# A graph layer's sparse sums: a ring of sums by edge type, with the weights applied when nodes leave it

## The chip, the cores and the metric

The kernel runs on one core of a Trainium2 chip. The metric is the device time of one execution, in microseconds (us). The engines are PE (TensorE: matrix products), DVE (VectorE), ACT (ScalarE), POOL (GpSimd, which here issues the indirect gathers) and SP (SyncE, which issues the plain DMAs). PEld is the loading of weights into PE. SBUF is the on-chip memory, of 128 partitions; PSUM holds PE's results, in banks that a pool hands out in turn.

## The reference

One layer of a typed graph network, cut to what matters:

```python
# x [12500, 128]; src, dst, edge_type [200000], edges sorted by dst
# W [4, 128, 128]; b [4, 128]
h = relu(layernorm(x))
xs = h[src]
for i in range(4):
    msgs += where(edge_type == i, xs @ W[i] + b[i], 0)
out = x + segment_sum(msgs, dst, N)
```

The destinations are drawn as the square of a uniform number, times 12500: the first nodes have hundreds of edges each, the last ones about eight.

## The kernel before, in words

**The table.** The kernel normalises x and stores h as a table `htab` in DRAM, as three bf16 pieces a row (384 bf16 values: `D3`), so that three bf16 products together carry an f32 value. This takes the first 99 us of the trace.

**Edges.** The 200000 edges, in order of destination, make 1563 chunks of 128. They are treated in three ways.

- *Dense.* The first 512 chunks (`C0`) belong to the first few hundred nodes. For them, `count` makes a matrix "how many edges go from this table row to this node and type": for each slot, DVE makes two one-hot matrices, `o1` (lines 943 and 947) and `o2` (line 948, 392 columns), PE multiplies them (line 959) and ACT writes the counts as fp8 (line 962). `multiply` then multiplies the whole table with the counts (line 999; the table comes in blocks of `HB` = 4 node columns, tile `hs`, through SP's queue), and its tail applies W and adds to `acc`, an SBUF array for the first 11 blocks of 128 nodes. There are 14 such batches, and the generator `dense_work` hands the work out in small steps.
- *Raw.* The first 3 groups (`RAW`) of 16 chunks after those are gathered from x itself (line 522) and normalised on the spot, while the table is still being made.
- *Sparse.* The other 1003 chunks come in groups of `G` = 16, with small groups of 12, 8, 4 and 3 at the end. POOL gathers 128 rows of the table per chunk with an indirect DMA (line 538, tile `hm`, two chunks to a buffer, 20 buffers). DVE makes a one-hot matrix `oh` (line 555) from type and destination: 4 types times a window of `win` destination nodes (10 to 26, growing along the edges, since later nodes have fewer edges).

**The sum of a sparse group** (`sum_up`, then `weigh`). Three matmuls a chunk (line 572: the three pieces of `hm` against `oh`) give, for the chunk, the sum of its rows by type and by node of the window. ACT copies these sums to SBUF (line 575). PE counts the edges by type and node (line 590), ACT casts the counts (line 594), and PE puts bias times counts (line 597) and W times sums, one f32 product per type over the whole group (line 599), into one PSUM bank. From there DVE adds each chunk's `win` columns into the ring (line 660), an SBUF array of `RING` = 2048 node columns (and 32 more for what hangs over), at an offset that is read from memory at run time.

**Nodes that leave.** When no later edge can reach a node block any more (`due`, `goes`), `put_out` empties it: `leave` fetches x for four blocks (`OT` = 4) by SP, transposes the ring's columns on PE (line 685), adds on DVE, stores through SP (line 694), and clears the ring's columns with a memset. The first 11 blocks go from the ring into `acc`, and leave at the end of the dense work.

**The order of the work.** PE, DVE and ACT run in the order in which the program is written out (`manual_schedule`). The loop over groups takes each group in parts of two chunks (`HG`). After each part, as much dense work is issued as `pace` says, by columns of PE work (`columns` estimates a group's), so that dense work lasts till nearly the end of the full groups. One-hots of the next group and ring additions of the group before (`side`) are dealt out over the parts. In `count`, one-hots are made `AHEAD` = 8 slots ahead of PE, from pools of 12 buffers each. Gathers of a group are issued one group ahead, on POOL's queue, as far as buffers are free.

Of the kernel before, what the change touches and what calls it, by code (L numbers as in the profile page):

```python
# [28 lines left out]

# [19 lines left out]
P = 128  # L49
EPS = 1e-5  # L50
UN = 3
G = 16
# [6 lines left out]
HB = 4  # L59
AHEAD = 8  # L60
BEHIND = 0.06
RING = 2048
OT = 4
# [3 lines left out]
SOON = (RAW * 16) + HG  # L67

# [4 lines left out]
def kernel(  # L73
# [148 lines left out]
    ring = const.tile([P, RING + WIN], F32, name="ring")  # L222
# [7 lines left out]
    hpool = mid.enter_context(tc.tile_pool(name="rows", bufs=20))  # L230
# [3 lines left out]
    s_ps = mid.enter_context(tc.tile_pool(name="s_ps", bufs=2, space=PSUM))  # L234
    y_ps = mid.enter_context(tc.tile_pool(name="y_ps", bufs=1, space=PSUM))
# [236 lines left out]
    banks = [(s_ps, "ps"), (s_ps, "ps"), (y_ps, "py"), (a_ps, "pa")]  # L472
# [87 lines left out]
    finish = []  # L560
    flushing = []

    def sum_up(t0, g, rows, oh, last):
        win = window_of(C0 + t0)
        K = NT * win
        sb = spool.tile([P, G * KM], F32, name="sb")[:, : G * K].rearrange("p (g t n) -> p g t n", g=G, t=NT)
        for i0 in range(0, g, SG):
            i1 = min(i0 + SG, g)
            ps = s_ps.tile([P, 512], F32, name="ps")[:, : SG * K].rearrange("p (i n) -> p i n", i=SG)
            for i in range(i0, i1):  # L570
                for c in range(3):
                    nc.tensor.matmul(ps[:, i - i0, :], rows(i, c), oh[:, i, :], start=(c == 0), stop=(c == 2))  # L572
                if i % HG and i + 1 < i1:
                    yield (i + 1) / g
            nc.scalar.copy(sb[:, i0:i1].rearrange("p g t n -> p g (t n)"), ps[:, : i1 - i0, :])  # L575
            yield i1 / g

        finish.append(weigh(t0, g, oh, sb, last))

    def weigh(t0, g, oh, sb, last):  # L580
        win = window_of(C0 + t0)

        def bank():
            to = x_ps.tile([P, G * WIN], F32, name="pt") if last else y_ps.tile([P, G * WIN], F32, name="py")
            return to[:, : G * win].rearrange("p (g n) -> p g n", g=G)

        ohv = oh.rearrange("p g (t n) -> p g t n", t=NT)
        pc = bank()
# [6 lines left out]
        yield True  # L595
        py = bank()
        nc.tensor.matmul(py[:, :g, :], b128, cnt[:, :g, :], start=True, stop=False)
        for t in range(NT):
            nc.tensor.matmul(py[:, :g, :], wsb[:, t, :], sb[:, :g, t, :], start=False, stop=(t == NT - 1))  # L599
# [873 lines left out]
```

## Time and profile before

| what | value |
| --- | --- |
| median of 3 runs | 1405.44 us (1405.35 to 1410.56) |
| the profiled execution's own time | 1402.26 us |
| its span in the profile | 1400.5 us |
| PE busy | 1314.0 us (94%) |
| DVE busy | 1002.7 us (72%) |
| ACT busy | 628.8 us (45%) |
| POOL busy | 1032.2 us (74%) |
| gathers of table rows (line 538) | 1003, mean 972 ns |
| one-hots `o2` (line 948) | 1167, mean 333 ns |
| table times counts on PE (line 999) | 4116, 892.2 us |
| sums of rows on PE (line 572) | 3009, 186.6 us |
| W on the sums (line 599) | 488, 130.7 us |
| copies of the sums on ACT (line 575) | 251, 100.3 us |
| ring additions on DVE (line 660) | 976, 167.8 us |

The profile records one execution. Busy time is the sum over an engine's instructions, so an engine can be busy without setting the pace, and an instruction's busy time can hold time in which it waits for the one ahead in its pipeline. Slices are 40 equal parts of the span, with busy shares in tenths. A line of the view of waits names who waited, behind the arrow what ended the idle time (the releaser; "issue" means that the engine waited for nothing that the profile shows), and then the idle time in us, how often, and the longest one. A line of the view by stretches has the stretch, its length, busy us and number of instructions of each engine (or of one program line alone), and at the end the clock granted to PE (1.00 is full), the DMA engines' busy share and GB/s. A line of the timeline has start, duration, engine, program line, operation, its tiles and, in brackets, the idle time before it and its releaser.

### The profile page before, as it was taken

The page shows a single profiled execution, that of the slowest core. Times are in us where ns is not written, and L with a number is a line of the kernel's source. Part 1 is how long each engine was busy: PE and PEld are TensorE (multiplying, and loading weights), DVE is VectorE, ACT ScalarE, POOL GpSimd, SP SyncE. Part 2 cuts the span into 40 slices and gives each one's busy share as a digit, 9 for nine tenths or more (in the row PEclk, how much of TensorE's full clock was granted, in tenths as well). Part 3 has the DMA queues.
Part 4 walks back from the last instruction along what each step waited for, and adds up shares of the span by engine and source line. Part 5 has one row for each costly group of instructions (what it writes and reads, how often), then busy time and mean ns, then how long its engine had stood idle before and what let it go on. Part 6 is the DMA issues. An engine that isn't in the chain of part 4 may idle for free.

```text
span 1400.5 us, 30850 instructions
## 1 busy us (share of the span) xinstructions
PE 1314.0 (94%) x9776; PEld 809.6 (58%) x9776; DVE 1002.7 (72%) x5153; ACT 628.8 (45%) x2043; POOL 1032.2 (74%) x1078
## 2 busy tenths in 40 slices
PE   4869888999999999999999999999999999999974
PEld 1437466565666666666666656666666655556543
DVE  9990999987887678776767767676777667753533
ACT  6795626244263535445353543535344353361111
POOL 7726777777777777777777777777777777777774
PEclk9995899999999999999999999999999999999977
DMA  8643466676667767676767666777677666767752
GB/s 249 220 172 81 115 193 204 182 219 172 202 186 217 213 202 213 204 220 198 212 190 222 199 202 201 207 208 208 187 208 206 193 199 184 207 189 205 215 146 68
DMA packets 143094, 270.27 MB, mean 193 GB/s; under 512 B 26602, under 2 KB 79004, under 8 KB 142925
## 3 DMA queue, kind: packets, MB, share of 16 engines
q1 hardware_dynamic: 93245, 166.45, 39.0%
q0 software_dynamic: 49680, 101.81, 26.8%
q8 instruction: 77, 1.26, 0.4%
q14 instruction: 92, 0.75, 0.2%
HBM read 252.12 MB, written 16.04 MB: 191 GB/s over the span
## 4 chain that ended last, share of the span: by engine, by line
PE 77%; DVE 10%; DMA 6%; issue 3%; POOL 2%; ACT 1%; SPq 0%; DVEq 0%; POOLq 0%; ACTq 0%
PE pa L999 45%; PE pt L959 12%; PE py L599 8%; PE ps L572 6%; DMA hm<-htab,srcT 5%; DVE o L948 2%; POOL hm L538 2%; DVE o L947 1%; PE ps L629 1%; DVE oh L555 1%; DVE ring L660 1%; DMA hm<-in_x_dram 1%; PE pt L685 1%; PE py L590 1%; PE pt L1015 1%
## 5 line engine op out<-in xcount | busy, mean ns | idle before, releaser
L538 POOL DMA_INDIRECT hm<-htab,srcT x1003 | 974.5, 972 | 332.6 <-issue 190.4
L999 PE MATMUL pa<-counts,hs 128*128 128x416 fp8e4 (+1 forms) x4116 | 892.2, 337 | 0.6 <-ACT sd L1009 0.6
L999 PEld LDWEIGHTS <-hs 128*128 128x128 bf16 x4116 | 391.4, 98 | 257.6 <-issue 1.9
L962 ACT ACTIVATE counts<-pt 128x392 uint16<-128x392 f32 x714 | 355.4, 507 | 342.6 <-PE pt L959 326.1
L948 DVE TENSOR_SCALAR o<-iota_n,hkT 128x392 bf16<-128x392 f16 x1167 | 388.1, 333 | 0.0
L959 PE MATMUL pt<-o,o 128*128 128x392 bf16 x1167 | 372.6, 334 | 10.1 <-DVE o L948 7.0
L555 DVE TENSOR_SCALAR oh<-iota_b,keyT 128x56 bf16<-128x56 bf16 (+8 forms) x1003 | 173.2, 264 | 185.4 <-PE py L590 182.6
L660 DVE TENSOR_TENSOR ring<-ring,py 128x14 f32 (+7 forms) x976 | 167.8, 172 | 95.5 <-PE py L599 46.2
L575 ACT COPY sb<-ps 128x224 f32<-128x224 f32 (+8 forms) x251 | 100.3, 400 | 295.4 <-PE ps L572 278.7
L572 PEld LDWEIGHTS <-hm 128*128 128x128 bf16 x3009 | 162.0, 98 | 101.2 <-DMA hm<-htab,srcT 28.9
L572 PE MATMUL ps<-oh,hm 128*128 128x56 bf16 (+8 forms) x3009 | 186.6, 197 | 23.4 <-DMA hm<-htab,srcT 21.5
L959 PEld LDWEIGHTS <-o 128*128 128x128 bf16 x1167 | 113.0, 98 | 78.9 <-DVE o L948 15.0
L947 DVE TENSOR_SCALAR o<-iota_b,loT,byT 128x128 bf16<-128x128 bf16 x417 | 139.6, 335 | 12.2 <-PE pt L959 10.4
L962 ACT ACTIVATION_READ_ACCUMULATOR counts<-pt 128x1 f32 x714 | 147.1, 206 | 0.0
L599 PE MATMUL py<-sb,wsb 128*128 128x224 f32 (+7 forms) x488 | 130.7, 412 | 0.0
L943 DVE TENSOR_SCALAR o<-iota_b,loT 128x128 bf16<-128x128 bf16 x375 | 98.2, 262 | 13.0 <-PE pt L959 12.7
L599 PEld LDWEIGHTS py<-sb,wsb 128*128 128x128 f32 x488 | 89.3, 196 | 25.3 <-issue 2.9
L947 DVE TENSOR_SCALAR o<-iota_b,loT 128x128 bf16<-128x128 bf16 x375 | 97.1, 259 | 8.2 <-PE pt L959 7.9
L522 POOL DMA_INDIRECT hx<-in_x_dram,srcT x48 | 52.1, 1086 | 19.6 <-issue 9.6
L594 ACT CAST cnt<-py 128x224 bf16<-128x224 f32 (+7 forms) x61 | 24.2, 396 | 56.6 <-PE py L590 56.6
L455 ACT ACTIVATE h<-hm,nmrt,rstdt 128x128 f32<-128x128 f32 x98 | 43.1, 502 | 0.8 <-DVE nmrt L450 0.5
L484 PE MATMUL ps<-h,ident 128*128 128x384 f32 (+1 forms) x34 | 16.7, 575 | 16.1 <-ACT h L455 16.0
(230 smaller groups left out, 601.8 us busy)
## 6 DMA issues: line engine op xcount, KB each, us to landing
hs<-htab SPq DMA_DIRECT2D x336, 384.0 KB
hm<-htab,srcT POOLq DMA_INDIRECT x1003
htab<-h SPq DMA_DIRECT2D x32, 288.0 KB
xo<-in_x_dram SPq DMA_DIRECT2D x23, 256.0 KB
out_dram<-xo SPq DMA_DIRECT2D x23, 256.0 KB
hm<-in_x_dram SPq DMA_DIRECT2D x18, 192.0 KB
hs<-htab SPq DMA_DIRECT2D x14, 192.0 KB
hm<-in_x_dram SPq DMA_DIRECT2D x14, 168.0 KB
```

The costliest lines, as they stand in the source:

```text
L538: one = nc.gpsimd.indirect_dma_start(out=hm[:, (i - h0) * D3 : (i - h0 + 1) * D3], out_offset=None, in_=htab, in_offset=bass.IndirectOffse ...
L555: nc.vector.tensor_scalar(oh[:, i, :], iota_b[:, :K], keyf[:, at : at + 1], None, ALU.is_equal)
L572: nc.tensor.matmul(ps[:, i - i0, :], rows(i, c), oh[:, i, :], start=(c == 0), stop=(c == 2))
L575: nc.scalar.copy(sb[:, i0:i1].rearrange("p g t n -> p g (t n)"), ps[:, : i1 - i0, :])
L599: nc.tensor.matmul(py[:, :g, :], wsb[:, t, :], sb[:, :g, t, :], start=False, stop=(t == NT - 1))
L660: nc.vector.tensor_tensor(to, to, of(i), ALU.add)
L943: nc.vector.tensor_scalar(o1, iota_b, loT[:, s : s + 1], None, ALU.is_equal)
L947: nc.vector.tensor_scalar(o1, iota_b, loT[:, s : s + 1], by, ALU.is_equal, ALU.mult)
L948: nc.vector.tensor_scalar(o2, iota_n, hkT[:, s : s + 1], None, ALU.is_equal)
L959: nc.tensor.matmul(pb, o1, o2, start=first, stop=last)
L962: nc.scalar.activation(counts[:, :, i * NT : (i + 1) * NT], pb.rearrange("p (b t) -> p b t", t=NT), AF.Copy, accum_out=both[:, i : i + 1],)
L999: nc.tensor.matmul(pa[:, : nv * NT], hs[:, j - j0, c * D : (c + 1) * D], counts[:, j, : nv * NT], start=(j == 0 and c == 0), stop=(j == NW ...
```

## The change

- The ring holds, for every node, the sums of h by type (4 planes) and the summed bias (a fifth plane), instead of one finished sum: `ring` becomes [128, 5, 1024 + 32] instead of [128, 2048 + 32].
- W is no longer applied to each group (`weigh` and its lines 590 to 599 go, with the copy of line 575). It is applied when a block leaves the ring: `from_ring` multiplies the block's four planes with the four W and the fifth with the identity, into one PSUM tile that stands where the transpose's result stood. Blocks leave in twos (`OT` = 2), at most one such pair per group, at the part `FLUSH` = 3.
- Bias times counts goes into the same PSUM bank as the chunk's sums (five planes of `win` columns a chunk). The counts of a group (`counts_of`) are made in the group before.
- DVE adds the five planes of a chunk with one instruction, straight from PSUM, two parts after PE has made them (`LAG` = 2). The pool of these banks gets a third bank; the bank for W's results goes.
- Row buffers: 16 pairs instead of 20.
- In `count`, one-hots lie in tiles of 4 slots (`SLOTS`), 4 tiles per kind, each made while the set two before it is multiplied; ring additions and one-hots of rows are dealt out between the steps of dense work, instead of behind all those of the part.
- The table is loaded in blocks of 7 node columns (`HB` = 7) in 3 buffers, instead of 4 in 4.
- `columns`, which feeds `pace`, counts the new work. The clearing of the ring covers five planes. The check of counts of a batch is dealt out in steps. The order at the end of the program is written anew.

The core of the diff:

```diff
-HB = 4
-AHEAD = 8
+HB = 7
+SLOTS = 4
-RING = 2048
-OT = 4
+RING = 1024
+OT = 2
+LAG = 2
+FLUSH = 3
...
-    ring = const.tile([P, RING + WIN], F32, name="ring")
+    ring = const.tile([P, NT + 1, RING + WIN], F32, name="ring")
...
-    hpool = mid.enter_context(tc.tile_pool(name="rows", bufs=20))
+    hpool = mid.enter_context(tc.tile_pool(name="rows", bufs=16))
-    s_ps = mid.enter_context(tc.tile_pool(name="s_ps", bufs=2, space=PSUM))
-    y_ps = mid.enter_context(tc.tile_pool(name="y_ps", bufs=1, space=PSUM))
+    s_ps = mid.enter_context(tc.tile_pool(name="s_ps", bufs=3, space=PSUM))
...
+    def counts_of(t0, g, oh):
...
+        nc.scalar.copy(cnt[:, :g], pc[:, :g])
+        return cnt
+
+    def sum_up(t0, g, rows, oh, cnt):
+        win = window_of(C0 + t0)
+        many = SG if SG * (NT + 1) * win <= 512 else HG
+        banks = []
+        each = ring_adds(
+            t0,
+            g,
+            lambda i: banks[i // many][0][:, i - banks[i // many][1]],
+            lambda at: ring[:, :, bass.ds(at, win)],
+        )
+        for i0 in range(0, g, many):
+            i1 = min(i0 + many, g)
+            ps = s_ps.tile([P, 512], F32, name="ps")[:, : many * (NT + 1) * win]
+            ps = ps.rearrange("p (i k n) -> p i k n", i=many, k=NT + 1)
...
+                if i % HG and i + 1 < i1:
+                    yield (i + 1) / g
+            nc.tensor.matmul(ps[:, : i1 - i0, NT, :], b128, cnt[:, i0:i1, :], start=True, stop=True)
+            banks.append((ps, i0))
+            adds.append(each[i0:i1])
+            yield i1 / g
...
+    def from_ring(j, r, to):
+        c = j * P % RING
+        for t in range(NT):
+            nc.tensor.matmul(to, ring[:, t, c : c + r], wsb[:, t, :], start=(t == 0), stop=False)
+        nc.tensor.matmul(to, ring[:, NT, c : c + r], ident, start=False, stop=True)
...
             if again:
-                nc.vector.memset(ring[:, c0 : c0 + n], 0.0)
+                nc.vector.memset(ring[:, :, c0 : c0 + n], 0.0)
...
+        for n, of in enumerate(sets):
+            while len(making) < min(n + 3, len(sets)):
+                making.append(make(sets[len(making)]))
+                made.append([])
+            ahead = [m for m in range(n, min(n + 2, len(sets)))]
+            for m in ahead:
+                made[m] += list(making[m])
+            for k, (i, s, by, first, last) in enumerate(of):
+                if n + 2 < len(sets) and len(made[n + 2]) < len(sets[n + 2]):
+                    made[n + 2].append(next(making[n + 2]))
...
-        return sizes[gi] * (3 * max(64, K) + 5 * K)
+        nodes = N * (((C0 + starts[gi] + sizes[gi]) / T) ** 2 - ((C0 + starts[gi]) / T) ** 2)
+        return sizes[gi] * (3 * max(64, K) + K + win) + 4 * (NT + 1) * nodes
...
-    hsp = counting.enter_context(tc.tile_pool(name="hsp", bufs=4))
+    hsp = counting.enter_context(tc.tile_pool(name="hsp", bufs=3))
...
+            flush = j == FLUSH and out_now
+            if flush:
+                while ready and ready[0][0] <= last_add:
+                    ready.pop(0)[1]()
+            lag, many = (LAG, HG) if gi < FULL else (1, SG)
+            some = [ready.pop(0)[1] for _ in range(many) if not flush and ready and ready[0][0] + lag <= at_part]
...
             while work and spent < pace(gi, part):
                 spent = next(work, None)
                 if spent is None:
                     work = None
+                if some:
+                    some.pop(0)()
...
+            if flush:
+                ending.append(put_out(*out_now.pop(0), True))
+            while adds:
+                ready.extend((at_part, add) for add in adds.pop(0))
```

## The prediction

> **What bounds the kernel now.** I read the page's busy shares and slices first, then the busy times by stretch, then who POOL waits for, then counts by line, then the timeline at the end.
>
> ```profile
> PE 1314.0 (94%) x9776; PEld 809.6 (58%) x9776; DVE 1002.7 (72%) x5153; ACT 628.8 (45%) x2043; POOL 1032.2 (74%) x1078
> PE   4869888999999999999999999999999999999974
> POOL 7726777777777777777777777777777777777774
> ```
>
> PE looks like the bound: nine tenths or more from slice 8 on. POOL looks idle a quarter of the time. The stretches show what that quarter is.
>
> ```profile
> 400.00:450.00 50.00, 50.00 (x405) 30.84 (x404) 38.84 (x210) 26.78 (x96) 38.13 (x40) 1.00 0.71 204
> 1000.00:1050.00 50.00, 50.00 (x377) 30.74 (x376) 36.60 (x187) 20.86 (x69) 38.12 (x40) 1.00 0.69 200
> 1300.00:1350.00 50.00, 44.32 (x317) 26.66 (x314) 25.45 (x149) 6.71 (x14) 37.84 (x40) 0.97 0.68 193
> ```
>
> Columns: length, then PE, PEld, DVE, ACT, POOL, each with its count. POOL issues 40 gathers in every 50 us, one in 1.25 us, also at the end where PE is no longer full. POOL's waits say that nothing holds it:
>
> ```profile
> POOL hm L538 <- issue: 190.4, 625, 0.3
> POOL hm L538 <- ACT rstdr L446: 21.5, 1, 21.5
> POOL hm L538 <- ACT hx L455: 8.0, 7, 4.6
> ```
>
> Of 1003 gathers nearly all have a gap of 0.3 us, whatever name it bears. Only the first (21.5 us, until the table is stored) and two more (1.9 and 4.6 us, held to the raw groups) really wait. From the first gather at 99.46 us to the last at 1384.18 us there are 1002 spacings of 1.25 us (1252 us), 6 us of those two waits, and 27 us of stretch (the group's mean of 972 ns against 945 ns, times 1003): 1285 us, all of the time there is. Gathers (first fence) and row matmuls, three a chunk (second), from the start to four moments:
>
> ```profile
> 0.00:270.00 270.00, 126.00 (x128) 0.89 0.59 176
> 0.00:400.00 400.00, 225.54 (x228) 0.93 0.62 183
> 0.00:860.00 860.00, 575.54 (x589) 0.97 0.67 195
> 0.00:1130.00 1130.00, 780.95 (x801) 0.97 0.68 197
> ```
>
> ```profile
> 0.00:270.00 270.00, 16.16 (x300) 14.95 (x300) 0.89 0.59 176
> 0.00:400.00 400.00, 32.50 (x612) 30.09 (x612) 0.93 0.62 183
> 0.00:860.00 860.00, 96.10 (x1734) 87.37 (x1734) 0.97 0.67 195
> 0.00:1130.00 1130.00, 138.39 (x2388) 124.36 (x2388) 0.97 0.68 197
> ```
>
> POOL is 28 chunks ahead of PE at 270 us, 24 at 400, 11 at 860, 5 at 1130: PE catches up long before the end, and from there waits for rows. The end is POOL's queue plus a tail:
>
> ```profile
> 1384.18 0.94 POOL L538 DMA_INDIRECT hm<-htab,srcT  x1 [0.30 <-issue]
> 1387.21 0.31 PE L572 MATMUL ps<-oh,hm 128*128 128x104 bf16 x3 [0.96 <-DMA hm<-htab,srcT]
> 1389.07 1.96 PE L599 MATMUL pt<-sb,wsb 128*128 128x78 f32 x8
> 1395.05 0.41 SPq L694 DMA_DIRECT2D out_dram<-xo  x1
> ```
>
> **The change part by part.** The profiled execution took 1402.26 us (span 1400.5); the median of the runs is 3.2 us above it. The sum is made against the first.
>
> W on leaving nodes, on PE. Removed: the L599 matmuls, 143 thousand columns over their forms; eight of 256 columns go from 706.82 to 708.55 us, 0.84 ns a column: 120 us. Removed too: 87 transposes (L685, four in 0.50 us): 10 us. Added: 87 blocks with ten f32 instructions each (W for four types and the identity, two passes each). Nearest row: L1015, 104 columns, eight in 0.88 us, 0.11 us each: 96 us. The bias goes from 61 wide matmuls (about 0.11 us) to some 250 narrow ones (0.033 us, as L572's 72 columns): +1 us. Net 33 us less PE work, 0.5 us a group of 16. What covers it is the gather queue: PE only catches up sooner. It is worth nothing to the end; it adds to a margin, since PE now gains about 0.7 us a group on POOL and reaches it some ten groups early.
>
> ACT loses 251 copies (L575, 100 us); ACT is 45% busy and off the path: 0.
>
> DVE. Each ring addition grows from win to 5 win columns. L660 takes 164 ns for 10 columns, L1025 210 ns for 58: about 1 ns a column, so 955 additions x 72 columns give +70 us. The clearing memsets grow from 20 of 512 columns (485 ns) to about 43 of up to 1280 (1408 columns took 1.23 us): +35 us. Against this the waits of oh for L590 (183 us) go, since the counts are made a group ahead. 1003 us becomes about 1110: no bound over the whole, but from 150 to 266 us DVE has no idle time at all. There it decides how far PE lags, and the row buffers fall from 20 to 16 pairs: POOL may be 32 chunks ahead, not 40. In this trace a limit of 16 would leave 2.5 us of slack at the tightest gather (the 114th), 4 to 6 us up to the 190th. I summed DVE's queue up to the one-hot that each chunk's matmuls stand behind, by start-to-start spacings of this trace (o2 0.231, o1 0.16 or 0.22, oh 0.142; a ring addition 0.202 behind another one, 0.08 behind another kind, plus 1.04 ns a further column). For the kernel before, this is within 2 us of the trace up to 270 us. For the changed order, where additions stand singly between one-hots, it comes 3.4 us later at chunk 16, 1 us at 64, 2 us at 96, 3 us at 128. Bounds: 0, and 7 us if single additions cost as much as those in a row (chunks then 6 to 11 us late, less the slack). I take +1, nearer the isolated rows.
>
> The stretch of the gathers. It comes with o2 (L948) alone: gathers with none starting beside them last 3 ns over 945, with one 21, two 39, three 105; runs of ring additions do nothing. In the built order, 750 of 885 runs of o2 are of one; before, most are of two and more (up to 19, as at 331 to 337 us, where gathers take 1.27 us). The count, 1167, stays. At 20 ns each that is 23 us instead of 27. Bounds: -10 (the o2 hardly meet gathers) and +5 (DVE, no longer held by L590, runs ahead and bunches). I take -3.
>
> [...]
>
> POOL's queue: the ring's memset goes from 2080 to 5280 columns (1.82 to about 4.6 us) and delays the 48 raw gathers; they end at 78 us, with 21.5 us idle after: 0; without that cover, 2.8 us. The raw groups get a third sum bank: they waited 2.3 us in all for copies, so the two held gathers may come sooner: between -2 and 0; I take -1.
>
> SP's queue: table loads of 7 blocks instead of 4 (350 loads become 196, same bytes), 45 fetches and 45 stores instead of 24. In the built order a load is released at least 8 us of PE work before its first use (6.5 us before), for 672 KB instead of 384 KB: at the 200 GB/s of the stretches 3.4 us instead of 1.9. No wait of PE for hs is in this trace; I take 0, bounds 0 and the margin below. Two fetches of x now stand ahead of the last table stores: their wait ends with a slot matmul (L851, last at 65.4 us), so they cost issue time, 0.43 us each; between 0 and 1, I take +0.5.
>
> The wait that is added: PE's flush stands behind DVE's additions of the group before, and DVE's clearing behind PE's flush. The first are emitted a part (2.5 us) or more earlier; behind the second stand one-hots that PE needs some three parts later: 0.
>
> The tail. Before, 7.8 us pass from the last rows (1387.2) to the last store. Removed: W, counts and copy of the last group (1387.4 to 1390.8). Added: 40 f32 matmuls for blocks 92 to 95, able to start at about 1384.5, ending 1388.9 (0.11 us each); the last rows' matmuls 0.7; five DVE additions, 1.9; 20 f32 matmuls, 2.2 us at full clock or 4.3 at half (L599's 78-column rows: 0.21 us); 0.5 for DVE. The store goes out at 1394.2 to 1396.5; with the 40 at half clock too, up to 4 us later. I take +1; bounds -1 and +5.
>
> Sum: +1 -3 -1 +0.5 +1 = -1.5 us: 1400.8 for the profiled execution, 1404 for the median.
>
> **The rivals.** *PE is the bound after all.* Then its 33 us come off: 1372. For it: 50.00 of 50. Against: POOL's rhythm is the same where PE has idle time. 0.05.
>
> *The stretch goes.* If spreading o2 takes most of the 27 us, 1385 or so; the gathers with no o2 show it possible, the constant count speaks against. If half goes, 1391. 0.11 for the two.
>
> *Sixteen pairs are too few* (the other side). If DVE between 140 and 300 us falls behind by more than the slack, POOL waits for a free buffer and never regains it. By additions at the price of a row it costs 7 us (1412); it decides over 0.5% from a lag of about 11 us at chunks 80 to 150. For it: DVE has no idle time there, and a ring addition has five times the columns. 0.14.
>
> *New waits eat PE's margin.* PE could lose about 40 us (33 plus what is left at 1130 us) before it bounds again; late loads of hs at each of 14 batches, 5 us each, give 70: 1435. 0.06. *The tail at half clock* with small losses elsewhere: 1413. 0.04.
>
> *The lock.* If single o2 each held a gather for half their length, 1167 x 0.76 (POOL's share) x 0.115 us = 102 us against 27: 1480. The gathers with one o2 now (21 ns) speak against. 0.02. [...]
>
> **How the numbers follow.** 0.5%, 7 us, is about what a measurement of this kernel tells from no change. The forecast, POOL's queue as before, holds 0.58, and all of it lies within 0.5%. Faster: 0.05 + 0.11 = 0.16. Slower: 0.14 + 0.06 + 0.04 + 0.02 = 0.26. The forecast's own bounds (-13 to +18 with every end at once) make 1397 to 1413 likely. The range of 1390 to 1418 takes in half of the stretch rival below, and the buffers' and the tail's above; it leaves out 0.05 + 0.05 + 0.06 + 0.02 = 0.18.
>
> **What would show it.** POOL still 40 gathers in 50 us, the last at about 1382 to 1386 us; PE idle in many slices, waiting for hm, from about 700 us; L599 and L575 gone, some 870 f32 matmuls at the flush; the group mean of L538 below 972 ns. Wrong would be: spacings of POOL over 1.3 us named after PE between 200 and 320 us (buffers), PE waits for hs, or a first gather later than 101 us.

## The result, and the profile after

The changed kernel takes 1418.1 us (median of 5 runs, 1416.4 to 1421.5) against 1405.4 us before: 1.0088 times as long, with a 95% interval of 1.0071 to 1.0105. Measured side by side a second time, it was 1.0091 (1.0069 to 1.0112). The forecast was 1404.0 us, no change beyond 0.5%; the time is 1% above it, and 0.1 us above the range given. The profiled execution took 1418.36 us, its span is 1416.6 us. In 8 of the 18 runs below, called stalled, every kernel took about 1.2 times as long (the one before 1680 to 1705 us), because the queue of gathers stopped 230 to 248 times for about 1.3 us, for a reason that no run shows; of these runs only counts within one trace and comparisons among themselves are used.

Lines of the program move a little: the gathers are L540 now, the row matmuls L592, the ring additions L662, the clearings L728, o2 L971. From the page of the changed kernel: busy times, and the slices of PE and POOL.

```profile
PE 1293.5 (91%) x10240; PEld 813.9 (57%) x10240; DVE 1056.5 (75%) x5250; ACT 547.2 (39%) x1792; POOL 1042.0 (74%) x1078
PE   4979888999999999999999999999999989999675
POOL 7626777777777777777777777777777777777773
```

PE has 20 us less to do, DVE 54 us more, ACT 82 us less. The prediction had PE stand in many slices waiting for rows; it is still at nine tenths. The same stretches as before, with the same columns:

```profile
400.00:450.00 50.00, 48.62 (x406) 29.60 (x405) 40.66 (x218) 24.39 (x86) 38.12 (x40) 1.00 0.66 206
1000.00:1050.00 50.00, 49.07 (x410) 31.57 (x408) 40.34 (x201) 15.61 (x53) 38.41 (x39) 1.00 0.64 197
1300.00:1350.00 50.00, 37.48 (x296) 23.84 (x295) 31.42 (x165) 0.96 (x2) 37.81 (x41) 0.87 0.63 197
```

POOL keeps its rhythm, with one gather missing between 1000 and 1050 us. PE now has holes: 12.5 us of them in the last line. Gathers and row matmuls (three a chunk) from the start to the four moments:

```profile
0.00:270.00 270.00, 124.59 (x128) 0.89 0.58 178
0.00:400.00 400.00, 223.31 (x230) 0.92 0.59 183
0.00:860.00 860.00, 574.79 (x586) 0.96 0.63 195
0.00:1130.00 1130.00, 780.87 (x796) 0.97 0.63 196
```

```profile
0.00:270.00 270.00, 16.30 (x306) 15.04 (x306) 0.89 0.58 178
0.00:400.00 400.00, 32.09 (x606) 29.58 (x606) 0.92 0.59 183
0.00:860.00 860.00, 94.98 (x1716) 85.61 (x1717) 0.96 0.63 195
0.00:1130.00 1130.00, 137.12 (x2370) 121.78 (x2370) 0.97 0.63 196
```

POOL leads by 26 chunks at 270 us, 28 at 400, 14 at 860, 6 at 1130. With 33 us less work PE was to catch up sooner than before (28, 24, 11, 5); it catches up later, although POOL is 5 gathers behind its old place at 1130 us. The waits, in us, times, longest:

```profile
POOL hm L540 <- issue: 221.2, 726, 0.3
PE ps L592 <- DVE ring L662: 50.9, 52, 2.7
POOL hm L540 <- ACT hx L457: 28.6, 8, 22.0
```

In the kernel before, PE's row matmuls waited for ring additions 1.2 us in all, and its matmuls of the counts (L590) 8.6 us:

```profile
PE ps L572 <- DMA hm<-htab,srcT: 21.5, 25, 3.1
PE py L590 <- DVE ring L660: 8.6, 4, 3.2
PE ps L572 <- DVE ring L660: 1.2, 2, 1.0
```

There PE waited 21.5 us for rows. Among the waits of the changed kernel's row matmuls none is for rows (3.9 us in its second trace): PE stays behind POOL to the end, and its own delay sets the end.

POOL is late as well, and its account closes: the first gather starts at 102.18 us (+2.7), the two early waits are 1.1 us shorter, the gathers are stretched by 36.2 us over 945 ns each instead of 26.7 (+9.5), the last one starts at 1395.32 us instead of 1384.18 (+11.1). From it to the end 21.3 us pass instead of 16.3 (+5.0). Together +16.1 us, the difference of the spans.

The stretch has two parts. From the starts and durations of the gathers and of the clearings (L728): 26 gathers that start while a clearing runs, or up to 0.22 us ahead of it, are stretched by 20.3 us together, the longest by 1.38 us; in the kernel before, no gather was stretched by more than 0.05 us under a clearing (8 started there). All other gathers are stretched by 16.0 us, against 26.7 us before. The timeline of one held gather, and of one that is not (start, duration, engine, line):

```profile
955.53 2.30 POOL L540 DMA_INDIRECT hm<-htab,srcT  x1 [0.30 <-issue]
...
955.71 1.12 DVE L728 MEMSET ring<- 128x1280 f32 x1 [0.21 <-DVE xo L690]
956.76 0.26 DVE L731 TENSOR_TENSOR ring<-ring 128x160 f32<-128x160 f32 x1
...
896.50 1.12 DVE L728 MEMSET ring<- 128x1280 f32 x1 [0.22 <-DVE xo L690]
897.66 0.26 DVE L662 TENSOR_TENSOR ring<-ring,ps 128x100 f32 x1
...
896.94 0.95 POOL L540 DMA_INDIRECT hm<-htab,srcT  x1 [0.30 <-issue]
```

The two clearings are alike (40 of the 42 have 1280 columns, two have 640). What differs is the DVE instruction behind them. At 956.76 it is the fold, recorded as starting 0.08 us before the clearing ends, so it was already lined up; the gather lasts 2.30 us. At 897.66 it is a ring addition, which waits for the clearing by a semaphore and starts 0.03 us after its end; the gather beneath lasts 0.95 us. (It differs in kind too: one of its operands lies in PSUM. These rows alone do not tell waiting from kind; the runs below do in part.) This divides all 42 clearings, each of which has a gather starting under it or just ahead of it: with an o2 (L971) next, 16 of 16 are held; with the fold next, 10 of 10; with a ring addition next, 0 of 16. And the end tells which instruction lets go: behind a clearing with an o2 next, the gather ends 0.945 us after a moment 13 to 22 ns before the clearing's end; with the fold next, 42 to 47 ns after it. The o2 ends 117 ns after the clearing, the fold 177 ns: the same 60 ns.

The holding begins while the wide instruction still stands behind its predecessor. The gather at 955.53 would, with its 0.945 us, have ended at 956.48, 0.28 us before the fold is recorded as starting; in 9 of the 26 that end would come ahead of the wide instruction's recorded start, by up to 0.31 us. What it is in the chip that holds the gather, no run shows.

At the end, the timeline after:

```profile
1395.32 0.94 POOL L540 DMA_INDIRECT hm<-htab,srcT  x1 [0.30 <-issue]
1396.10 0.62 DVE L662 TENSOR_TENSOR ring<-ring,ps 128x130 f32 x2 [0.42 <-PE ps L601]
1396.77 2.07 PE L704 MATMUL pt<-wsb,ring 128*128 128x128 f32 x8 [0.71 <-DVE ring L662]
1403.89 0.44 PE L592 MATMUL ps<-oh,hm 128*128 128x104 bf16 x6
1404.19 0.30 PE L592 MATMUL ps<-oh,hm 128*128 128x104 bf16 x3
1409.62 0.50 SPq L694 DMA_DIRECT2D out_dram<-xo  x1
```

The last rows are summed 8.9 us after the last gather's start; before, it was 3.0 us. From there to the end it takes 12.4 us, before 13.3. So the tail itself is not longer: PE is late on the last rows. Part of that is the 40 f32 products of blocks 92 to 95, 7.1 us from 1396.77 to 1403.89, the first eight at twice the time of later ones (2.07 us against 1.06); the clock granted to PE from 1397 to 1404 us is 0.63 (0.50 from 1396 to 1402, 0.96 from 1402 to 1404). Part is older. Two views show a hole in PE, by the timeline, and what DVE did then, by the tile `low` of both kernels (count, durations in ns, first and last start); first the changed kernel:

```profile
1346.47 0.64 PE L592 MATMUL ps<-oh,hm 128*128 128x96 bf16 x6 [12.52 <-DVE oh L557]
```

```profile
L776 DVE TENSOR_TENSOR low<-low,step x44: 169/170/172, 1326.1 to 1343.9; 128x9 f32<-128x9 f32 x44
```

```profile
L753 DVE TENSOR_TENSOR low<-low,step x23: 170/171/192, 1310.4 to 1319.7; 128x9 f32<-128x9 f32 x23
```

This is `check_chunks`: for each set of blocks that leaves together, two short instructions that wait for one another, 0.41 us a set, all in one piece at the end of group 61. With blocks leaving in twos there are 44 sets, 18 us. Before, there were 23, 10 us, and PE lost 0.4 us by them. PE's clock falls around the hole as well: it is 0.60 from 1335 to 1347 us and 0.50 from 1347 to 1350, against 0.90 and 0.84 in the kernel before; what this costs was not measured by itself.

### The profile page after: what moved, and what is told of

Its sections match the earlier page's. It is cut to its first block, busy times and chain, and to the rows that moved or that the text cites. A ratio compares the mean times of both kernels' runs of the same rounds, so it can differ in the third digit from the quotient of the medians.

```text
span 1416.6 us, 31450 instructions
## 1 busy us (share of the span) xinstructions
PE 1293.5 (91%) x10240; PEld 813.9 (57%) x10240; DVE 1056.5 (75%) x5250; ACT 547.2 (39%) x1792; POOL 1042.0 (74%) x1078
## 4 chain that ended last, share of the span: by engine, by line
PE 64%; DVE 27%; issue 3%; ACT 2%; DVEq 2%; DMA 1%; SPq 0%; POOL 0%; ACTq 0%; POOLq 0%
PE pa L1044 36%; PE pt L996 9%; DVE o L971 7%; PE pt L704 6%; PE ps L592 6%; DVE o L977 4%; DVE ring L662 4%; DVE oh L557 3%; DVE o L973 2%; DVEq L653 2%; DVE ring L728 2%; PE pt L705 1%; DVE xo L690 1%; PE ps L631 1%; ACT h L457 1%
## 5 line engine op out<-in xcount | busy, mean ns | idle before, releaser
L540 POOL DMA_INDIRECT hm<-htab,srcT x1003 | 984.1, 981 | 332.1 <-issue 221.2
L971 DVE TENSOR_SCALAR o<-iota_n,hkT 128x392 bf16<-128x392 f16 x1167 | 381.2, 327 | 3.6 <-PE pt L996 3.1
L662 DVE TENSOR_TENSOR ring<-ring,ps 128x70 f32 (+8 forms) x1003 | 241.8, 241 | 29.1 <-PE ps L601 8.6
L557 DVE TENSOR_SCALAR oh<-iota_b,keyT 128x56 bf16<-128x56 bf16 (+8 forms) x1003 | 234.5, 259 | 26.8 <-PE ps L601 18.0
L592 PE MATMUL ps<-oh,hm 128*128 128x56 bf16 (+8 forms) x3009 | 183.4, 198 | 65.1 <-DVE ring L662 50.9
L592 PEld LDWEIGHTS <-hm 128*128 128x128 bf16 x3009 | 160.6, 99 | 142.9 <-issue 86.1
L690 DVE TENSOR_TENSOR xo<-pt,xo 128x256 f32<-128x256 f32 (+2 forms) x51 | 20.8, 412 | 207.7 <-PE pt L705 207.7
L704 PE MATMUL pt<-wsb,ring 128*128 128x128 f32 (+1 forms) x696 | 95.6, 282 | 4.5 <-DVE ring L662 4.5
L704 PEld LDWEIGHTS pt<-wsb,ring 128*128 128x128 f32 (+1 forms) x696 | 90.4, 198 | 7.9 <-DVE ring L662 5.0
L573 ACT CAST cnt<-pt 128x320 bf16<-128x320 f32 (+9 forms) x65 | 25.1, 386 | 150.4 <-PE pt L569 150.0
L728 DVE MEMSET ring<- 128x1280 f32 (+1 forms) x42 | 46.2, 1100 | 8.9 <-DVE xo L690 8.6
L601 PE MATMUL ps<-cnt,b 128*128 128x56 bf16 (+8 forms) x258 | 51.0, 198 | 0.0
```

What stands on the lines that cost most here:

```text
L540: one = nc.gpsimd.indirect_dma_start(out=hm[:, (i - h0) * D3 : (i - h0 + 1) * D3], out_offset=None, in_=htab, in_offset=bass.IndirectOffse ...
L557: nc.vector.tensor_scalar(oh[:, i, :], iota_b[:, :K], keyf[:, at : at + 1], None, ALU.is_equal)
L592: nc.tensor.matmul(ps[:, i - i0, :NT, :].rearrange("p k n -> p (k n)"), rows(i, c), oh[:, i, :], start=(c == 0), stop=(c == 2),)
L662: nc.vector.tensor_tensor(into, into, of(i), ALU.add)
L704: nc.tensor.matmul(to, ring[:, t, c : c + r], wsb[:, t, :], start=(t == 0), stop=False)
L728: nc.vector.memset(ring[:, :, c0 : c0 + n], 0.0)
```

## The experiments

Two theories were set against each other in the runs. *P*: POOL's queue alone sets the end, so what the holds cost comes off if they go. *Q*: PE, which now waits for DVE, is as late as POOL, so that each cure alone gains little. A second pair concerns the holds: *1*, a wide DVE instruction lined up behind the clearing holds the gather; *2*, the clearing itself does, in two of three cases.

**The floor of the kernel before.** The kernel before, less work on PE:

```diff
         for t in range(NT):
-            nc.tensor.matmul(py[:, :g, :], wsb[:, t, :], sb[:, :g, t, :], start=False, stop=(t == NT - 1))
+            if t < 1:
+                nc.tensor.matmul(py[:, :g, :], wsb[:, t, :], sb[:, :g, t, :], start=False, stop=True)
```

> The kernel before with W applied for one edge type instead of four in the sparse groups (the other three are left out): some 90 us less work on PE. If POOL's queue sets the time of the kernel before, as the prediction has it, only the tail gets shorter: 1403 to 1405, ratio 0.998 to 1.000. If PE is the bound, 1315, ratio 0.94. If both are near the bound, the last gather stays within 2 us of 1384.

1405.82 us, ratio 1.0004 (0.9995 to 1.0014). PE is busy for 62 us less (some 90 were expected) and waits for rows instead:

```profile
PE 1251.9 (89%) x9386; PEld 744.4 (53%) x9386; DVE 997.0 (71%) x5153; ACT 630.1 (45%) x2043; POOL 1031.5 (74%) x1078
...
PE ps L572 <- DMA hm<-htab,srcT: 86.0, 117, 2.7
```

So the gather queue was the floor of the kernel before, as the prediction read it. (The last gather came at 1387.4, 3.2 us later, with a first one 0.9 us later and 2.3 us more stretch.)

**The changed kernel again**, as the base for what follows:

> The changed kernel itself, beside the kernel before on one chip. Where gathers come 1.25 us apart, as in the two traces at hand: 1.0088 times the kernel before, last gather 11 us later, 26 gathers held under the clearings. Where the queue of gathers stalls on its own (as on the chip of the first four experiments, with 250 waits of about 1.2 us each), POOL's stretch is hidden behind these stalls, and what is left of the loss is the start, the tail and PE's waits for ring additions: 1.010 to 1.016 times before.

1418.3 us, ratio 1.0091; last gather at 1394.5, 26 gathers held for 18.8 us. As expected.

**A reduction behind each clearing.**

```diff
                 nc.vector.memset(ring[:, :, c0 : c0 + n], 0.0)
+                nc.vector.tensor_reduce(mark, ring[:, 0, c0 : c0 + 2], AX.X, ALU.max)
```

> The changed kernel with a two-column reduction of the cleared columns behind each clearing of the ring, so that no wide one-hot (o2) or fold stands queued on DVE directly behind a clearing; the clearings themselves stay as they are. Theory 1 (a wide DVE instruction that is queued behind the clearing holds the gather until it has ended): the 26 gathers that were held for 20 us in all become 0 to 3, and the group mean of the gathers falls from 981 to about 961 ns. Theory 2 (the clearing itself holds the gather, by chance in two of three cases): 26 of 40 are held as before, mean 981 ns. For the time: if POOL alone sets the end (theory P), 20 us less, 1398; if PE, which waits 36 us for ring additions around the clearings, is as late as POOL (theory Q), POOL's last gather comes up to 20 us earlier but the time falls only by 2 to 5 us, 1413 to 1416.

> The changed kernel with the two-column reduction behind each clearing, again. Theory 1: no gather held under a clearing. Where gathers come 1.25 us apart: theory P (POOL alone sets the end) 20 us below the changed kernel, ratio to before about 0.995; theory Q (PE as late as POOL) 2 to 5 us below it, ratio 1.005 to 1.008.

The first of the two is a stalled run, the second is not. Both show no held gather (0 of 43 and 0 of 48 under a clearing): theory 1. But the time of the second is 1459.4 us, ratio 1.0377 (1.0359 to 1.0394), 41 us more than the changed kernel. Neither theory had that. PE's waits for ring additions rose from 64.0 us in the changed kernel's second run to 97.9 us, its idle time after 140 us from 85 to 118 us, and POOL, 29 us ahead of PE at the end, waited 48 us for buffers. What the DVE queue did, listed from the trace with its register loads (start, duration in ns; the load brings the ring rows of the next group), changed kernel above, with the reduction below:

```
935.371   425 TENSOR_TENSOR L690      935.387  1097 TENSOR_LOAD L653
936.010  1125 MEMSET        L728      937.170   259 TENSOR_TENSOR L662

955.724   425 TENSOR_TENSOR L690      956.366  1125 MEMSET      L728
957.525   154 TENSOR_REDUCE L729      957.539  1099 TENSOR_LOAD L653
958.835   260 TENSOR_TENSOR L662
```

The load takes 1.10 us. In the changed kernel it starts beside the addition to x, 0.62 us ahead of the clearing, and ends 0.48 us into it (so at 30 of the 42 clearings; at the 10 with the fold next it starts 0.23 us behind the clearing's end). The reduction waits for the clearing and starts 0.03 us after its end, and in this listing nothing behind it on DVE starts sooner; the load comes 0.05 us after the clearing's end: the first ring addition comes 2.47 us after the clearing's start instead of 1.16.

**The counter-dose**: a wide one-hot that nothing uses behind each clearing.

```diff
                 nc.vector.memset(ring[:, :, c0 : c0 + n], 0.0)
+                nc.vector.tensor_scalar(spare, iota_n[:, :288], cidx[:, 0:1], None, ALU.is_equal)
```

> The changed kernel with one more one-hot of 288 columns (not used by anything) directly behind each of the clearings of the ring. Theory 1 (what is queued behind the clearing holds the gather): nearly every clearing under which a gather starts now holds it, about 40 gathers instead of 26, 31 us instead of 20; mean of the gathers about 992 ns. Theory 2 (the clearing itself): 26 and 20 us as before, mean 981 to 984 ns.

39 gathers held, of 41 under a clearing. This is a stalled run, and the holds sum to 11.9 us, not to the 31 expected; in the stalled run with only the tail altered (below), 26 of 42 are held, for 10.0 us. Theory 1 again; theory 2 falls with both.

**A reduction that waits for nothing.**

```diff
                 nc.vector.memset(ring[:, :, c0 : c0 + n], 0.0)
+                nc.vector.tensor_reduce(mark, rowf[:, :2], AX.X, ALU.max)
```

> The changed kernel with a two-column reduction of an old constant behind each clearing of the ring: it waits for nothing, so DVE's sequencer can still issue the load of the next ring rows (1.10 us) beside the clearing, which the reduction of the cleared columns had kept until after it. Theory 1 (only a wide instruction that is next in DVE's queue behind the clearing holds a gather): 0 to 3 gathers held, 18 to 20 us of holds gone. The loss of the waiting reduction (41 us against the changed kernel) is gone too if it was the exposed load: PE's idle time after 140 us falls from 118 back to 80 to 88 us. Time: 1398 if POOL alone sets the end; 1411 to 1416 if PE, late by its wait of 12.5 us at 1334 us and by the flushes, sets it together with POOL.

0 gathers held of 46; PE's idle time is 85 us again, so the exposed load was the 41 us. The last gather starts at 1377.9 us, 17 us earlier. And the time is 1416.4 us, ratio 1.0077 (1.0060 to 1.0094): 2 us less. PE's last rows come 24.6 us behind the last gather. Theory Q: the holds are some 19 us on POOL and hardly anything on the end, because PE is just as late. The group of gathers and PE's wait, with the waiting reduction and with the one that waits for nothing (both waits count the hole at the check, 13 us, which the trace of the changed kernel puts down to `oh`):

```profile
L540 POOL DMA_INDIRECT hm<-htab,srcT x1003 | 964.8, 962 | 375.4 <-issue 227.3 <-PE ps L592 52.0 <-PE pt L998 39.6
...
PE ps L592 <- DVE ring L662: 97.9, 63, 12.9
```

```profile
L540 POOL DMA_INDIRECT hm<-htab,srcT x1003 | 966.1, 963 | 333.6 <-issue 220.3 <-PE pt L998 29.8 <-ACT hx L457 28.7
...
PE ps L592 <- DVE ring L662: 66.2, 56, 13.0
```

**The check dealt out**: the loop over leaving blocks becomes a generator, one pair of instructions in every second part from group 21 on.

```diff
-        for (ja, jb, _), i in zip(flushes, goes):
+    def add_low():
...
+                nc.vector.tensor_add(low, low, step)
+                yield True
...
             at_part += 1
+            if gi > 20 and j % 2:
+                next(lows, None)
```

> The changed kernel with the loop over the leaving blocks in check_chunks (84 short DVE instructions in a row, 17 us, behind which PE stands idle for 12.5 us at 1334 us) dealt out over parts of groups 21 to 32, two instructions at a time. If this lump is why PE is 9 us behind the gathers at the end (3 us in the kernel before): PE's idle stretch at 1334 us goes, dense work ends near 1350 instead of 1363.6, the last gather stays at 1394 to 1396, and from it to the end 16 to 18 us pass instead of 21: 1412 to 1415. If POOL's holds and the f32 products of the tail are all there is: unchanged, 1417 to 1419.

The 12.5 us hole is gone, and dense work ends at 1354.7 instead of 1363.6. But 1417.0 us (1.0072, 1.0056 to 1.0089) is 1 us less, not 3 to 6: POOL, still held, gives its last gather at 1396.4, and PE, only 4.6 us behind at chunk 976, falls to 7.5 us by the 40 products ahead of the last rows. PE waits for rows again:

```profile
PE ps L592 <- DMA hm<-htab,srcT: 13.2, 12, 2.5
```

**The tail**: blocks 92 to 95 leave as soon as no later edge can reach them.

```diff
-            next((i for i in [*range(from_here, FULL), final - 1] if starts[i] + sizes[i] >= c), final)
+            next((i for i in range(from_here, final) if starts[i] + sizes[i] >= c), final)
...
-        if gi == final - 1:
+        if FULL <= gi < final:
+            for end in before_last:
+                end()
```

> The changed kernel with node blocks 92 to 95 leaving after the groups that end at chunks 1036 and 1044, as soon as no later edge can reach them, instead of both after chunk 1048. If the 40 f32 products at half clock ahead of the last rows are what made the tail 5 us longer: 1418 becomes 1412 to 1414, and from the last gather to the end about 16 to 17 us instead of 21.3. If PE is late by itself at the end (theory Q), the products only move and about 1416 to 1418 stays.

Its one run is a stalled one: 1725.8 us beside 1705.1 for the kernel before. It says nothing of the time at 1.25 us a gather; what the tail is worth there by itself was not measured.

**Three cures together** (reduction without a wait, check dealt out, tail):

> The changed kernel with three edits together: the reduction without a wait behind each clearing, the loop of check_chunks dealt out, and node blocks 92 to 95 leaving after chunks 1036 and 1044. If holds (18 to 20 us on POOL), the lump (12.5 us on PE) and the tail are the whole loss, and neither engine is free without the other: 1397 to 1403, ratio to before 0.994 to 0.999. If PE's remaining waits at the flushes (some 35 us) bind by themselves: 1405 to 1412.

1408.1 us, ratio 1.0016 (1.0006 to 1.0027). 10 us are gained where the first two alone gained 2 and 1. It is above the first range and within the second: PE still waits 56.3 us for ring additions, and its last rows come 14.4 us behind the last gather.

**The clearing cut into planes**, one in each of five parts:

```diff
-                nc.vector.memset(ring[:, :, c0 : c0 + n], 0.0)
+                clears.extend(lambda k=k: clear(k, c0, n) for k in range(NT + 1))
...
+            if clears and not flush:
+                some.append(clears.pop(0))
```

> The changed kernel with each clearing of the ring cut into its five planes, one plane (256 columns) in each of the five parts that follow, each with the two-column reduction behind it. Theory P (POOL alone sets the end): as with the reduction alone, about 1398 to 1402. Theory Q (PE as late as POOL, by its waits for ring additions that stand behind a 1.1 us clearing): PE's waits for ring additions between 250 and 1340 us fall from 36 us to under 12, dense work ends 20 us or so earlier than at 1363.6, and only now the time falls, to 1396 to 1404, below what the reduction alone gives.

> The changed kernel with the clearing cut into planes with the reduction behind each, POOL's clearing of the ring moved behind the raw gathers, and node blocks 92 to 95 leaving after chunks 1036 and 1044. Where gathers come 1.25 us apart: first gather back at 99.5 us (-2.7), 20 us of holds gone, 16 to 18 us from the last gather to the end (-4): 1390 to 1395, ratio 0.990 to 0.993. By theory Q the gain needs PE's waits for ring additions to go as well, which the cut clearings do; if they do not go, 1408.

> As the three edits together, and each clearing cut into its five planes, one in each of the five parts that follow, each with the reduction that waits for nothing. If PE's waits at the flushes come from the 1.1 us clearing ahead of the ring additions, PE's idle time after 140 us falls by another 15 to 25 us and the time is 1388 to 1397. If they come from the load of the ring rows (1.10 us) and the addition to x, cutting gains nothing over the three edits.

The first of these three is a stalled run (1730.4 us, 0 held). The second, with a waiting reduction behind each of the 210 cleared planes, took 1438.0 us (1.0220, 1.0200 to 1.0240) where 1390 to 1395 was expected. The same exposed load as above is the likely reason (PE waits 75.0 us for ring additions, 15.0 of them in the hole at the check). Its first gather at 102.5 us says that POOL's clearing of the ring, which it moved, is not what makes the start late. The third, with the three cures and reductions that wait for nothing, is the fastest: 1399.0 us (7 runs, 1394.4 to 1404.8; 1388 to 1397 was expected), ratio 0.9957 (0.9937 to 0.9978) to the kernel before, 1.3% below the changed kernel. Its trace is of the fastest of the seven executions. PE's wait and the end:

```profile
PE ps L593 <- DVE ring L663: 40.7, 51, 2.1
```

```profile
1375.57 0.95 POOL L540 DMA_INDIRECT hm<-htab,srcT  x1 [0.30 <-issue]
1379.41 0.30 PE L593 MATMUL ps<-oh,hm 128*128 128x104 bf16 x3
1385.79 0.41 SPq L695 DMA_DIRECT2D out_dram<-xo  x1
```

PE's last rows are 3.8 us behind the last gather, about as in the kernel before (3.0). Cutting the clearing took 15.6 us of PE's waits and 6 us of its idle time, less than the 15 to 25 us expected; the rest of the waits at the flushes stays.

**One thing undone in this version.** First the version itself, and three undone; these four are stalled runs (the base took 1691.1 us).

> The kernel with the cut clearings and the three edits once more, as the base for the next three: 1394 to 1402, ratio 0.993 to 0.998, POOL's last gather at 1375 to 1377, PE's last rows 3 to 5 us behind it.

> The base with the one-hots of a set of four slots made at once, as a run of four pairs on DVE, instead of one pair per slot between other work; same instructions, same count. If spreading the wide one-hots (o2) is what lowered the rest of the gathers' stretch (26.7 us in the kernel before, 16 to 18 us after the change, 14.7 us in the base): it rises by 8 to 14 us and, since POOL sets the end of the base, the last gather comes 8 to 14 us later and the time is 1405 to 1412. If the fall has another reason: unchanged.

> The base with the loop of check_chunks back in one piece at the end of group 61. PE stands idle for 12 to 15 us near 1325 us. In the base PE is 17 us behind the gathers at chunk 950 and 11 us at 976, and has 7 us of that made good by the last rows; with the lump the last rows are 8 to 13 us later: 1406 to 1412. If POOL alone set the end: unchanged.

> The base with node blocks 92 to 95 leaving after chunk 1048 again, so that 40 f32 products stand ahead of the last rows on PE. They took 7.1 us after the change (1396.8 to 1403.9), part of it at half clock: from the last gather to the end 21 us instead of 17, 1402 to 1406. If they had only been waiting for PE's lag: unchanged.

Against 1691 us for the base: 1698 with the one-hots in runs, 1703 with the check in one piece, 1694 with the old tail. The stretch rose from 10.5 to 19.6 us with the runs. Two of them also have a run with gathers 1.25 us apart. One puts the old `check_chunks` back; the other makes the one-hots of a set at once:

```diff
-                if n + 2 < len(sets) and len(made[n + 2]) < len(sets[n + 2]):
-                    made[n + 2].append(next(making[n + 2]))
+                if n + 2 < len(sets) and k == 0:
+                    made[n + 2] += list(making[n + 2])
```

> The base (cut clearings and the three edits) with the one-hots of a set made as a run, again. Where the queue of gathers stalls on its own, the stretch rose from 10.5 to 19.6 us. Where gathers come 1.25 us apart: stretch 22 to 27 us instead of 14.7, last gather at 1383 to 1389 instead of 1375.6, ratio to before 1.001 to 1.006 instead of 0.996. If the spreading is not what lowered the stretch: 0.996.

> The base with the loop of check_chunks back in one piece, again. Where gathers come 1.25 us apart: PE idle for 12 to 15 us near 1325 us, last gather unchanged at 1375 to 1378, last rows 8 to 13 us later than in the base, ratio to before 1.001 to 1.005 instead of 0.996. If POOL alone sets the end of the base: 0.996.

With runs: stretch 24.1 us instead of 14.9, as expected, so making wide one-hots in runs stretches the gathers, and spreading them accounts for most of the fall from 26.7 to 16 us. The time is 1427.0 us (1.0127, 1.0110 to 1.0144), 28 us above the base and more than expected. The last gather is 17.8 us later, of which 9 are stretch and 8 are waits for buffers that PE frees late: its waits for ring additions rise from 41 to 66 us. With the check in one piece: PE idle for 14.3 us at 1325 us, last gather unchanged at 1376.7, and 1416.1 us (1.0058, 1.0041 to 1.0076), 17 us above the base. PE does not make the hole good: it is 17.7 us behind the gathers at chunk 930, 31.6 at 950 and still 24.8 at the last one. I had expected 8 to 13 us.

Last gather, last rows and span are of the profiled execution, the ratio is of the medians:

| kernel | last gather, us | last rows behind it | span | ratio to before |
| --- | --- | --- | --- | --- |
| before | 1384.2 | 3.0 | 1400.5 | 1 |
| changed | 1395.3 | 8.9 | 1416.6 | 1.0088 |
| holds removed | 1377.9 | 24.6 | 1414.7 | 1.0077 |
| check dealt out | 1396.4 | 7.5 | 1416.2 | 1.0072 |
| these two and the tail | 1376.4 | 14.4 | 1404.0 | 1.0016 |
| and the clearing cut | 1375.6 | 3.8 | 1392.6 | 0.9957 |
| the same, check in one piece | 1376.7 | 24.8 | 1414.7 | 1.0058 |
| the same, one-hots in runs | 1393.3 | 19.5 | 1428.1 | 1.0127 |

## Why the prediction was wrong, step by step

Two steps failed. The waits that the change adds for PE ("ACT loses 251 copies" and "the wait that is added") were put at 0, and PE's row matmuls waited 51 us for ring additions. The stretch of the gathers was put at -3 us and came out at +9.5. A third cost, the check of the ring, stood in no term. Of the prediction's own signs, the last gather (1382 to 1386 us; it came at 1395.3), PE's waits for hm and a group mean below 972 ns (it is 981) failed, and a sign of being wrong came: the first gather at 102.2 us, later than 101.

- *What bounds the kernel before*: right. With 62 us less of PE the time stayed within 0.1%, and PE's wait for rows grew to 86 us.
- *W on leaving nodes*: the size of what was added was right, the conclusion not. The 870 f32 matmuls follow each other 0.11 us apart, 97 us (96 forecast). PE's busy time fell by 20 us, not by 33; no run shows where the difference went. But "it adds to a margin" failed: PE's idle time after 140 us rose from 45 to 83 us, which is more than the 33 us that were to be saved.
- *ACT loses 251 copies: 0*, and *the wait that is added: 0*. The copies cost nothing on ACT, but they freed PE's row banks. Without them a bank comes free when DVE has added it to the ring, and a longer delay of DVE reaches PE: 51 us of waits of the row matmuls where there had been 1.2 (and 8.6 of the counts' matmuls). The sentence on the added wait named PE's flush and DVE's clearing and found one-hots behind them; the ring additions, which stand there too, were left out. That the missing copies are the cause is read from the releasers in the traces; no run puts the copies back. What the waits cost in time is known in part: cutting the clearings took 15.6 us of them and 9 us of time.
- *DVE*: the two sizes right (additions +74 us, +70 forecast; clearings 46 us against about 11, +35 forecast), though DVE's busy time came to 1057 us and not to 1110; the place wrong. I priced the clearings as DVE time. At 1.1 us each they delay ring additions, and so PE; and gathers are held under them.
- *The check of the ring*: not in the sum at all. Halving `OT` doubled the flushes that its loop runs over; 18 us of DVE in one piece stopped PE for 12.5 us, late, where PE has no time to make it good (17 us of time in the run that puts it back into the fastest version).
- *The stretch of the gathers, -3*. The part that I reasoned about went further than forecast, from 26.7 to 16.0 us (-10.7 where -4 was worked out and -10 was the bound), by the spreading, as the run with one-hots in runs shows for most of it (9 us). The part that I did not see, 20.3 us under the clearings, made it +9.5. By itself this cost was hidden: without the holds the time is 2 us less, because PE is late too. The kernel before could not show it: its clearings had narrow one-hots, ring additions or a fold of 32 columns behind them. In the trace of the changed kernel the end of a held gather moves with the end of the wide instruction (117 or 177 ns after the clearing's), and comes up to 1.38 us late. The rival of the lock priced every single o2 at half its length, weighted with POOL's busy share; but in the trace of before, the 345 gathers with an o2 at work 150 ns after their start carry 91% of the stretch, 70 ns each, and the others 4 ns each, and for a moment 400 ns after the start the share is 48%. So in that trace the stretch goes with an o2 at work early in the gather, not with one at any moment of it.
- *Sixteen pairs*: right, barely. One wait of 0.6 us at 363 us. The tight place was later than forecast: gathers 200 to 206, at 363 to 370 us, start 0.3 to 0.5 us after the matmuls that free their buffers.
- *POOL's queue and the raw groups*: -1.1 us for the early waits (-1 forecast). The start is 1 to 3 us later in all versions of the changed kernel (first gather 101.1 to 102.5 us against 99.5 and 100.3 for the kernel before). It isn't POOL's larger clearing (the run that moves it starts at 102.5). What it is stays open.
- *SP's queue, hs*: right; PE has no wait for a table load.
- *The tail, +1*: +5.0. After the last rows it is 0.9 us shorter; PE comes to them 5.9 us later, by the 40 products, the first of them at half clock (0.50 from 1396 to 1402 us; forecast as a bound), and by PE's lag.
- *The rivals*: the one that came true in its mechanism is "new waits eat PE's margin", given 0.06. Its threshold, about 40 us, was nearly reached (38 us more idle time); its place, late loads of hs, was wrong, and so was its price (1435). The forecast itself was half of the truth: POOL's last gather and PE's last rows are both late, and the time moves by more than 2 us only when both are mended.

What stays open: the later start; how PE's remaining 41 us of waits in the fastest version divide between the load of ring rows and the addition to x; and what the tail and PE's lower clock at the end cost by themselves.

## What to carry to other kernels

A copy by an idle engine can be worth nothing as work and much as a decoupling: before taking it out, ask who frees the buffer in its place, and what that engine does in long pieces. When a floor is set by one queue and another engine has just caught up with it, price the change on both: here a cure on one side alone showed 0.1%, and four edits on both sides together 1.3%. A constant such as the number of blocks that leave together runs through every loop over them; look for the loops that aren't dealt out.

## What the runs showed of the hardware that I had not expected

- In these traces a wide DVE instruction (a one-hot of 392 or 288 columns by tensor_scalar, or a fold of 160 columns with both operands in SBUF) that was lined up behind a clearing of 1.1 us held an indirect gather of POOL for the rest of the clearing as well: in the changed kernel 16 of 16 with an o2 next, by up to 1.16 us (the o2 took 0.2 us), and 10 of 10 with a fold of 0.26 us next, by up to 1.38 us. A two-column reduction in between that waits for nothing ended this (0 of 46, 1 of 46 and 1 of 87 gathers held; 26 of 43 without it; 39 of 41 with a wide one always there). What makes an instruction wide enough is not settled: in the kernel before, three one-hots of 128 columns and two folds of 32 columns behind shorter clearings (0.17 and 0.49 us) held none.
- With a DVE instruction behind the clearing that waited for it on a semaphore, DVE's next register load (1.10 us) came 0.05 us after the clearing's end in the listing above; in the changed kernel it started 0.62 us ahead of the clearing at 30 of 42. With such a wait behind each of the 42 clearings the kernel took some 42 us longer (1459.4 us with a reduction that waits, 1416.4 us with one that does not).
